# Local layers of a fused transformer block on one core: k projected ahead of q, two small operations moved from POOL to DVE, and the output block moved behind the scores

## The chip, the core and the metric

The kernel runs on one core of a Trainium2 chip. A core has five engines that work through their own queues: TensorE (PE) for matrix products and transposes, VectorE (DVE), ScalarE (ACT), GpSimd (POOL), and SyncE (SP), which here only issues DMAs. An instruction starts when those before it in its queue allow it and when the semaphores it waits for are set, so one late instruction holds everything behind it in the same queue. The metric is the device time of one execution in microseconds; the time before is 1243.0 us, the median of three runs (1241.72 to 1243.09).

## The reference

The input is x of 4 x 1024 x 128 in fp32. Two blocks follow each other, each with an attention part and a feed-forward part under an adaptive layer norm. Block 0 has a linear attention and a routed mixture of 16 experts; the attention of block 1 looks at a window of 64 keys and a prefix of 16. The change touches the feed-forward part of block 1, which is itself a stack of two small transformer layers with local attention (8 heads of 64, window 64). Cut to what matters:

```python
for l in range(2):
    h = shift_token(x)
    q, k, v = split(h @ wqkv[l])                       # 3 x 512 columns, 8 heads of 64
    q = q / clip(norm(q), 1e-12) * q_scale[l]
    k = k / clip(norm(k), 1e-12) * k_scale[l]
    q, k = rotary_xpos(q, k)                           # q*cos + rotate_half(q)*sin, scaled by position
    sim = einsum("bhwid,bhwjd->bhwij", q * 8, look_around(k))
    attn = softmax(where(mask, -max, sim))
    x = x + (attn @ look_around(v)) @ wo[l]
    h = layernorm(shift_token(x)) * ln_g[l] + ln_b[l]
    a, g = split(h @ w1[l] + b1[l])
    x = x + (a * gelu(g)) @ w2[l] + b2[l]
```

The l2 norm of every head is what the change is about: a sum of 64 squares for each token and head, a maximum with a small number, and a power of -1/2.

## The kernel before

The tokens are cut into tiles of 128, eight to a sequence, so the two local layers have 2 x 4 x 8 = 64 tiles. They run from about 579 us to the end. Ahead of them come block 0 (to about 330 us) and the window attention of block 1 (to about 579 us); in the last iterations of the latter the first three tiles of the local layers are projected already, one of six projections (three tiles, q and k) per iteration (line 821).

PE's order is the order of the program (`manual_schedule(engines={PE})`). The order on DVE, ACT and POOL is planned at build time: an instruction goes into its engine's queue when the planner thinks it ready, earlier ones in the program first. So the queues of these three follow the program loosely, and moving a line can reorder them.

A tile of the local layers goes through these functions:

- `project` (line 645; w = 0 is q, w = 1 is k): PE multiplies 128 tokens with 512 columns (L653). ACT squares the result (L656), DVE makes two products, `co` with the cosines (L658) and `si` with the sines (L663), and sums the squares by head into `ss[:, w]` (L665, 128x8). POOL adds `co` and `si` (L673). When w is 1, POOL also takes the maximum of both halves of `ss` (L668, 128x16), raises them to -1/2 (L669, 128x16), and multiplies k's `co` by k's half (L675). The eight squared norms of q and of k so share one power, taken when the second of them, k, is there. q's half is not multiplied into q; it is the scale in the masking of the scores (L892).
- `turn`: PE transposes q or k (L845); ACT copies q to `qT` (L852), DVE copies k into `kT` (L858). For the first sequence of the first layer (`light`), q's sum is left to PE, which adds two products with the identity (L849).
- `values`: PE projects v (L864), ACT copies it, and SP shifts it by half a tile with two DMAs into `ve`.
- `scores`: 32 small products (L885); DVE masks them, scales them by q's half of `ss`, and keeps each row's least value (L892, eight instructions); ACT takes the exponentials and their sums (`exps`, L904).
- `over_sums`: DVE takes the reciprocals (L912); POOL normalizes one half of the weights and DVE the other (L919).
- `flip`: PE transposes the weights (L926), ACT copies them to `pt` (L928).
- `outputs`: PE multiplies them with v and `ve` (L940, 32 products), ACT copies the result to `os` (L944).
- Side steps, spread over the iterations: the projection of the outputs (`project_out`, L951), the layer norm in front of the MLP (`mlp_in`, `mlp_out`), and the MLP (`mlp_gate` L986, `mlp_up` L995 and L997, `mlp_down` L1003).

PE's matmul results lie in eight banks: two for scores, six for everything else in the local layers. A bank is free again when its last reader is done.

In iteration g of the loop (line 1064) PE's order is: scores of tile g, q's projection of tile g+2, first flip of tile g-2, k's projection of tile g+2, second flip of tile g-2, turn of q of tile g+1, outputs of tile g-3, turn of k of tile g+1, then side steps and the values of tile g-1. For 1 < g < 7 the turn of q stands ahead of the first flip.

Every layer norm goes through `ln_in` (line 133): DVE takes mean and variance (L144, L146) and subtracts the mean (L150); POOL adds epsilon to the variance (L152, 128x4), raises to -1/2 (L153) and multiplies (L154). There are 49 of them in the whole kernel, most of them in block 0 and the window attention.

Of the kernel before, what the change touches and what calls it, by code (L numbers as in the profile page):

```python
# [22 lines left out]
ALU = mybir.AluOpType  # L23
# [3 lines left out]
P = 128  # L27
# [9 lines left out]
HEADS, DH, DEPTH = 8, 64, 2  # L37
# [11 lines left out]
def adaln_blocks(ctx: ExitStack, tc: tile.TileContext, a: dict, out: bass.AP):  # L49
    nc = tc.nc  # L50
    pe, act, dve, pool = nc.tensor, nc.scalar, nc.vector, nc.gpsimd
# [4 lines left out]
    def const(name, shape, dtype=F32):  # L56
        return cp.tile(shape, dtype, tag=name, name=name)
# [5 lines left out]
    def bc(ap, shape):  # L63

        return ap.unsqueeze(len(ap.shape)).to_broadcast(shape)
# [39 lines left out]
    nhalf = const("nhalf", [P, 4])  # L105
# [27 lines left out]
    def ln_in(tp, src, wp, name, bufs=None, n=4):  # L133

        if src is not None:
            for i in range(4):
                pe.transpose(tp[:, i, :], src[:, i * P : (i + 1) * P], ident)
        tps = tp if isinstance(tp, list) else [tp]
        h, w = len(tps), D // len(tps)
        st = wp.tile([P, 4, 2, 6], F32, tag="st", name=f"st_{name}")  # L140
        mv = wp.tile([P, 4, 2], F32, tag="mv", name=f"mv_{name}")
        for i in range(n):
            for e in range(h):
                dve.bn_stats(st[:, i, e, :], tps[e][:, i, :])  # L144
        for i in range(n):
            dve.bn_aggr(mv[:, i, :], st[:, i, 0:h])  # L146

        xh = wp.tile([P, 4, D], F32, tag="xh", name=f"xh_{name}", bufs=bufs)
        for e in range(h):
            dve.tensor_tensor(xh[:, 0:n, e * w : (e + 1) * w], tps[e][:, 0:n], mv[:, 0:n, 0:1].to_broadcast([P, n, w]), ALU.subtract)  # L150
        rv = wp.tile([P, 4, 1], F32, tag="rv", name=f"rv_{name}")
        pool.tensor_scalar(rv[:, 0:n], mv[:, 0:n, 1:2], 1e-5, None, ALU.add)  # L152
        pool.tensor_tensor(rv[:, 0:n], rv[:, 0:n], nhalf[:, 0:n].unsqueeze(2), ALU.pow)  # L153
        ln_in.last = pool.tensor_tensor(xh[:, 0:n], xh[:, 0:n], rv[:, 0:n].to_broadcast([P, n, D]), ALU.mult)  # L154
        return xh
# [53 lines left out]
    NG8 = B * NT  # L209
# [390 lines left out]
    def const1(name, shape):  # L600
        return c1.tile(shape, F32, tag=name, name=name)

    wl = []
    for l in range(DEPTH):
        w = [const1(f"wqkv_{l}", [P, 3, HEADS * DH]), const1(f"wo_{l}", [P, 4, D]), const1(f"w1_{l}", [P, 2 * HID]), const1(f"w2_{l}", [P, 3, D])]
# [38 lines left out]
    late = {}  # L644
    pj = ctx.enter_context(tc.tile_pool(name="pj", bufs=3))

    def project(l, b, t, w, ps):


        nt = f"{l}_{b}_{t}_{w}"  # L650
        if w == 0:
            late[l, b, t, "ss"] = pj.tile([P, 2, HEADS], F32, tag="ss", name=f"ss_{nt}", bufs=4)
        pe.matmul(ps, lhsT=hs[l, b][:, t * P : (t + 1) * P], rhs=wl[l][0][:, w, :], start=True, stop=True)  # L653
        ph = ps.rearrange("p (h e) -> p h e", e=DH)
        sq = pj.tile([P, HEADS, DH], F32, tag="sq", name=f"sq_{nt}", bufs=2)
        act.activation(sq, ph, AF.Square)  # L656
        co = pj.tile([P, HEADS, DH], F32, tag=f"co{w}", name=f"co_{nt}")
        dve.tensor_tensor(co, ph, abs_[l][:, 0, t, w, :].unsqueeze(1).to_broadcast([P, HEADS, DH]), ALU.mult)  # L658
        si = pj.tile([P, HEADS, DH], F32, tag="si", name=f"si_{nt}", bufs=3)

        ex = bass.AP(tensor=ps.tensor, offset=ps.offset + 32, ap=[ps.ap[0], [DH, HEADS], [-32, 2], [1, 32]])
        sn = abs_[l][:, 1, t, w, :].rearrange("p (i e) -> p i e", i=2).unsqueeze(1).to_broadcast([P, HEADS, 2, 32])
        dve.tensor_tensor(si.rearrange("p h (i e) -> p h i e", i=2), ex, sn, ALU.mult)  # L663
        ss = late[l, b, t, "ss"]
        dve.tensor_reduce(ss[:, w, :], sq, AX.X, ALU.add)  # L665
        if w == 1:

            pool.tensor_scalar(ss, ss, 1.0e-24, None, ALU.max)  # L668
            pool.tensor_tensor(ss, ss, nhalf[:, 0:2].unsqueeze(2).to_broadcast([P, 2, HEADS]), ALU.pow)  # L669
        if w == 0 and light(l, b, t):  # L670
            late[l, b, t, "si"] = si
        else:
            pool.tensor_tensor(co, co, si, ALU.add)  # L673
        if w == 1:
            pool.tensor_tensor(co, co, bc(ss[:, 1, :], [P, HEADS, DH]), ALU.mult)  # L675
        late[l, b, t, "co", w] = co

    def light(l, b, t):

        return (l, b) == (0, 0) and t >= EARLY  # L680
# [5 lines left out]
    with (  # L686
# [28 lines left out]
        def weights(b, t):  # L715

            sv, mx = kept1[b, t, "s"]
            for j in range(4):
                if (b, t) != (0, 0):
                    maximum(b, t, j)  # L720
                mj = mx[:, 4 * j : 4 * j + 4]
                pr = kept1[b, t, "pr", j] = wp.tile([P, 4, KV], F32, tag="pr", name=f"pr_{b}_{t}_{j}", bufs=8)
                if j < 3:
                    dve.tensor_tensor(pr, sv[j], bc(mj, [P, 4, KV]), ALU.add)
                    act.activation(pr, pr, AF.Exp)
                else:
                    for h in range(4):
                        act.activation(pr[:, h, :], sv[j][:, h, :], AF.Exp, bias=mj[:, h : h + 1])
# [61 lines left out]
        def when(g, f, *args):  # L790
            if 0 <= g < NG8:
                f(*divmod(g, NT), *args)

        for g in range(-1, NG8 + 2):
            b, t = divmod(g, NT)
            ahead = 0 <= b and b + 1 < B
            if g == -1:
                weights(0, 0)
            when(g + 2, scores)
            when(g + 2, weights)  # L800
            if ahead and t in (2, 4):
                queries(b + 1, t // 2 - 1)
            for after, k, f in ((6, 0, tokens), (8, 0, normed), (11, 1, tokens), (13, 1, normed)):
                if (g - after) % NT == 0 and 0 <= (g - after) // NT < B - 1:
                    f((g - after) // NT, k, "h3")
            for at, k, f in ((1, 0, tokens), (3, 0, normed), (5, 1, tokens), (7, 1, normed)):
                if g == at:
                    f(B - 1, k, "h2")
            when(g - 1, back)
            when(g + 1, flip, (0, 1))  # L810
            when(g + 1, values)
            when(g, outputs)
            when(g + 1, flip, (2, 3))
            if t == 5 and 0 < b <= DEPTH:
                rotary(tab, abs_[b - 1], b - 1)
            if g % 4 == 1 and g > 4:
                project_out((g - 5) // NT, (g - 5) % NT // 4)
            if ahead and t in (3, 5):
                keys(b + 1, t // 2 - 1)

            for i, w in ((0, 0), (0, 1), (1, 0), (1, 1), (2, 0), (2, 1))[max(0, g - NG8 + 6) : max(0, g - NG8 + 7)]:
                project(0, 0, i, w, ps.tile([P, BLK], F32, tag="t", name=f"qk_0_0_{i}_{w}", bufs=2))

    both.close()
# [4 lines left out]
    with (  # L829
# [198 lines left out]
        for l in range(DEPTH):  # L1028
            for b in range(B):
                g = (l * B + b) * NT  # L1030
# [29 lines left out]
        def project_mid(l, b, t, w):  # L1060
            if (l, b) != (0, 0) or t >= EARLY:
                project(l, b, t, w, pM.tile([P, BLK], F32, tag="mid", name=f"qk_{l}_{b}_{t}_{w}"))

        for g in range(-1, tiles + 4):
            side = steps.get(g, [])
            when(g, scores)
            when(g + 2, project_mid, 0)

            turns = {-1: (0, 1), 0: (2,), 1: ()}.get(g, (g + 1,))
            if 1 < g < NT - 1:  # L1070
                when(g + 1, turn, 0)
            when(g - 2, flip, 0)
            when(g - 1, over_sums)
            when(g + 2, project_mid, 1)
            when(g - 2, flip, 1)
            when(g, exps)
            for i in turns:
                if not 1 < g < NT - 1:
                    when(i, turn, 0)
                if i < EARLY and g < EARLY:  # L1080
                    when(i, turn, 1)
            when(g - 3, outputs)
            if g >= EARLY - 1:
                when(g + 1, turn, 1)
            for f, args in side[:1]:
                f(*args)

            for i in {0: (), 1: (0,)}.get(g, (g - 1,)):
                when(i, values)

            f0 = g - 7
            if f0 % 4 == 0 and 0 <= f0 < tiles - NT:
                lo = f0 % NT * P
                project_out(f0 // (B * NT), f0 // NT % B, lo, lo + BLK)
            for f, args in side[1:]:
                f(*args)
# [127 lines left out]
```

## Time and profile before

| | us |
|---|---|
| time before, median of three runs | 1243.0 |
| the profiled execution | 1246.33 |
| its span | 1244.5 |
| block 0 | 0 to about 330 |
| window attention | about 330 to 579 |
| local layers, start | 579 to 692 |
| local layers, steady part | 692 to 1193 |
| last tiles and last MLP blocks | 1193 to 1244.5 |

One profiled execution gives a page and a trace of all its instructions. In the page, the first lines give the busy time of each engine with its share of the span; PEld is the loading of weights, which overlaps with PE. The groups of instructions read: line, engine, operation, result <- operands, shapes, how often; then the busy time in us and the mean of one in ns; then how long the engine sat idle just before them and what ended that. The busy time by stretch gives, for a window of the span, how long each engine was busy in it. The chain of waits is followed back from the end: each piece is an instruction that the next one waited for, by a semaphore or because it stood ahead of it in its queue. The timeline has every instruction with its start and its duration in us.

### The profile page before, as it was taken

To read this page: it belongs to the slowest core of one execution; us is meant where nothing else is said; L and a number is where in the kernel's file an instruction comes from. 1 tells how busy PE (TensorE), PEld (TensorE's weight loads), DVE (VectorE), ACT (ScalarE), POOL (GpSimd) and SP (SyncE) were. 2 spreads that over 40 slices of the span, in tenths; PEclk is the share of its full clock that TensorE was granted. 3 is DMA by queue.
4 is the path that set the end of the run, shared out by engine and by line. 5 is a ranking of instruction groups with operands and counts; after the bars stand their busy time and mean duration, and the time that the engine had idled before them with its cause. 6 is when DMAs were issued, how large, how long until landed. Compare 5 with 4: busy or idle time off the path is not lost.

```text
span 1244.5 us, 34772 instructions
## 1 busy us (share of the span) xinstructions
PE 1162.8 (93%) x13578; PEld 714.7 (57%) x13578; DVE 878.8 (71%) x2798; ACT 817.8 (66%) x2223; POOL 823.3 (66%) x813
## 2 busy tenths in 40 slices
PE   6789999999899999988898999999999999999998
PEld 5644453534476667755665556665555556565564
DVE  5556263452476667666878988898898888998864
ACT  3363373322577677766886788788877887788862
POOL 4436445746334445444889988888899889888840
PEclk8699999999999999999999999999999999999999
DMA  6040404021400000000112111111111111111110
GB/s 179 1 130 8 138 0 132 7 74 63 137 4 4 3 20 14 11 3 3 35 27 48 27 35 26 32 40 27 39 28 34 39 29 45 38 27 31 36 40 26
DMA packets 36136, 51.04 MB, mean 41 GB/s; under 512 B 5850, under 2 KB 17668, under 8 KB 35844
## 3 DMA queue, kind: packets, MB, share of 16 engines
q1 hardware_dynamic: 35540, 48.29, 14.1%
q8 instruction: 107, 1.75, 0.6%
q10 hardware_dynamic: 432, 0.53, 0.1%
q14 instruction: 57, 0.47, 0.1%
HBM read 26.52 MB, written 2.36 MB: 23 GB/s over the span
## 4 chain that ended last, share of the span: by engine, by line
PE 43%; DVE 27%; ACT 18%; POOL 7%; issue 5%; DMA 1%; POOLq 0%; ACTq 0%; SPq 0%; DVEq 0%
ACT pr L904 5%; PE h L489 4%; PE yp L951 4%; DVE pr L892 3%; DVE co L658 3%; PE s L885 3%; DVE si L663 3%; DVE ss L665 3%; PE ptr L735 3%; PE qk L653 3%; POOL u L494 2%; ACT sq L656 2%; PE s L261 2%; PE obank L752 2%; DVE ge L997 2%
## 5 line engine op out<-in xcount | busy, mean ns | idle before, releaser
L904 ACT ACTIVATE pr<-pr,mx 128x128 f32<-128x128 f32 x512 | 200.8, 403 | 88.2 <-DVE mx L892 88.1
L673 POOL TENSOR_TENSOR co<-co,si 128x512 f32<-128x512 f32 x123 | 156.7, 1280 | 79.5 <-DVE si L663 72.2
L669 POOL TENSOR_TENSOR ss<-ss,nhalf 128x16 f32<-128x16 f32 x64 | 191.7, 2995 | 5.3
L892 DVE CUSTOM_DVE_ANT_0 pr<-s,masks,ss 128x128 f32<-128x128 f32 x512 | 144.2, 342 | 42.4 <-PE s L885 42.0
L653 PE MATMUL qk<-wqkv,hs 128*128 128x512 f32 x256 | 137.7, 620 | 4.9 <-ACT pt L737 4.9
L494 POOL TENSOR_TENSOR u<-u,cw 128x512 f32<-128x512 f32 x64 | 81.1, 1271 | 74.4 <-ACT u L492 74.4
L489 PE MATMUL h<-hT,w 128*128 128x512 f32 x256 | 123.8, 605 | 4.0 <-DVE g L496 4.0
L496 DVE TENSOR_TENSOR g<-u,h 128x512 f32<-128x512 f32 x64 | 43.8, 686 | 114.9 <-POOL u L494 114.9
L279 DVE TENSOR_REDUCE mx<-s 128x4 f32<-128x448 f32 x128 | 73.5, 617 | 56.4 <-PE s L270 56.4
L658 DVE TENSOR_TENSOR co<-qk,ab 128x512 f32<-128x512 f32 x128 | 86.7, 677 | 26.0 <-ACT sq L656 26.0
L904 ACT ACTIVATION_READ_ACCUMULATOR pr<-pr,mx 128x1 f32 x512 | 101.7, 199 | 0.0
L492 ACT ACTIVATE u<-h 128x512 f32<-128x512 f32 x64 | 38.2, 598 | 93.2 <-PE h L489 85.7
L926 PEld LDWEIGHTS ptr<-ident,pr 128*128 128x128 f32 x512 | 63.5, 141 | 61.6 <-issue 54.8
L663 DVE TENSOR_TENSOR si<-qk,ab 128x512 f32<-128x512 f32 x128 | 86.8, 678 | 0.0
L489 PEld LDWEIGHTS h<-hT,w 128*128 128x128 f32 x256 | 48.3, 194 | 66.2 <-issue 51.0
L665 DVE TENSOR_REDUCE ss<-sq 128x8 f32<-128x512 f32 x128 | 86.2, 673 | 0.0
L656 ACT ACTIVATE sq<-qk 128x512 f32<-128x512 f32 x128 | 74.9, 586 | 14.8 <-PE qk L653 12.3
L845 PE MATMUL qktr<-ident,co 128*128 128x128 f32 x492 | 76.9, 280 | 6.6 <-POOL co L675 5.3
L885 PEld LDWEIGHTS s<-kT,qT 64*64 64x64 f32 x2048 | 56.8, 134 | 45.6 <-issue 22.1
L919 POOL TENSOR_TENSOR pr<-pr,sm 128x512 f32<-128x512 f32 x64 | 74.7, 1168 | 7.9 <-DVE sm L912 7.9
L885 PE MATMUL s<-kT,qT 64*64 64x128 f32 x2048 | 72.1, 277 | 7.6 <-DVE kT L858 6.1
L737 ACT COPY pt<-ptr 112x512 f32<-112x512 f32 x128 | 72.5, 612 | 8.6 <-PE ptr L735 8.6
(212 smaller groups left out, 2871.2 us busy)
## 6 DMA issues: line engine op xcount, KB each, us to landing
cw<-cd SPq DMA_DIRECT2D x128, 128.0 KB, 3.0
ve<-vs SPq DMA_DIRECT2D x120, 128.0 KB, 2.3
hs<-hT SPq DMA_DIRECT2D x16, 256.0 KB, 3.2
out<-out SPq DMA_DIRECT2D x7, 256.0 KB, 2.7
xin<-in_x SPq DMA_DIRECT2D x3, 512.0 KB, 6.1
w<-in_w SPq DMA_DIRECT2D x3, 512.0 KB, 5.0
wqkv<-in_wqkv SPq DMA_DIRECT2D x2, 768.0 KB, 5.3
ab<-in_tab SPq DMA_DIRECT2D x1, 1024.0 KB, 7.3
```

Source lines behind the costliest of these rows:

```text
L489: pe.matmul(h, lhsT=w[:, c * P : (c + 1) * P], rhs=hT[b][:, blk(k)], start=True, stop=True)
L494: pool.tensor_tensor(u, u, kept[b, k, "cw"][:, c, :], ALU.mult)
L653: pe.matmul(ps, lhsT=hs[l, b][:, t * P : (t + 1) * P], rhs=wl[l][0][:, w, :], start=True, stop=True)
L656: act.activation(sq, ph, AF.Square)
L658: dve.tensor_tensor(co, ph, abs_[l][:, 0, t, w, :].unsqueeze(1).to_broadcast([P, HEADS, DH]), ALU.mult)
L663: dve.tensor_tensor(si.rearrange("p h (i e) -> p h i e", i=2), ex, sn, ALU.mult)
L665: dve.tensor_reduce(ss[:, w, :], sq, AX.X, ALU.add)
L669: pool.tensor_tensor(ss, ss, nhalf[:, 0:2].unsqueeze(2).to_broadcast([P, 2, HEADS]), ALU.pow)
L673: pool.tensor_tensor(co, co, si, ALU.add)
L885: pe.matmul(S[j][qs, c, :], lhsT=q[rw, c, qs], rhs=k[rw, c, at : at + P], start=True, stop=True)
L892: dve.tensor_tensor_reduce(out=pr[:, c, :], in0=S[j][:, c, :], in1=mk[:, min(t, 1), :], scale=kept[l, b, t, "ss"][:, 0, h : h + 1], scalar ...
L904: act.activation(pr[:, c, :], pr[:, c, :], AF.Exp, bias=mx[:, j, c : c + 1], scale=-1.0, accum_out=sm[:, j, c : c + 1])
```

## The change

It does five things.

1. In `project`, the maximum moves from POOL to DVE and is taken for each half by itself, directly after the sum of squares (128x8, in place of one 128x16 on POOL). The power is taken for each half by itself, too (128x8): k's ahead of the sum of `co` and `si`, q's behind it.
2. k is projected ahead of q, in the loop of the local layers and for the three tiles that are projected early. The tile `ss` is made by whichever comes first.
3. `outputs` of tile g-3 moves from behind the turn of q to directly behind the scores of tile g.
4. So PE's order in iteration g becomes: scores of tile g, outputs of tile g-3, k's projection of tile g+2, first flip, q's projection, second flip, turn of q, turn of k, side steps, values.
5. In `ln_in`, the addition of epsilon moves from POOL to DVE.

```diff
@@ ln_in
         rv = wp.tile([P, 4, 1], F32, tag="rv", name=f"rv_{name}")
-        pool.tensor_scalar(rv[:, 0:n], mv[:, 0:n, 1:2], 1e-5, None, ALU.add)
+        dve.tensor_scalar(rv[:, 0:n], mv[:, 0:n, 1:2], 1e-5, None, ALU.add)
@@ project
-        if w == 0:
+        if (l, b, t, "ss") not in late:
             late[l, b, t, "ss"] = pj.tile([P, 2, HEADS], F32, tag="ss", name=f"ss_{nt}", bufs=4)
...
         dve.tensor_reduce(ss[:, w, :], sq, AX.X, ALU.add)
+        dve.tensor_scalar(ss[:, w], ss[:, w], 1.0e-24, None, ALU.max)
         if w == 1:
-
-            pool.tensor_scalar(ss, ss, 1.0e-24, None, ALU.max)
-            pool.tensor_tensor(ss, ss, nhalf[:, 0:2].unsqueeze(2).to_broadcast([P, 2, HEADS]), ALU.pow)
+            pool.tensor_tensor(ss[:, 1], ss[:, 1], nhalf[:, 0:1].to_broadcast([P, HEADS]), ALU.pow)
         if w == 0 and light(l, b, t):
             late[l, b, t, "si"] = si
         else:
             pool.tensor_tensor(co, co, si, ALU.add)
         if w == 1:
             pool.tensor_tensor(co, co, bc(ss[:, 1, :], [P, HEADS, DH]), ALU.mult)
+        else:
+            pool.tensor_tensor(ss[:, 0], ss[:, 0], nhalf[:, 0:1].to_broadcast([P, HEADS]), ALU.pow)
@@ the early projections
-            for i, w in ((0, 0), (0, 1), (1, 0), (1, 1), (2, 0), (2, 1))[max(0, g - NG8 + 6) : max(0, g - NG8 + 7)]:
+            for i, w in ((0, 1), (0, 0), (1, 1), (1, 0), (2, 1), (2, 0))[max(0, g - NG8 + 6) : max(0, g - NG8 + 7)]:
@@ the loop of the local layers
             when(g, scores)
-            when(g + 2, project_mid, 0)
+            when(g - 3, outputs)
+            when(g + 2, project_mid, 1)
...
             when(g - 1, over_sums)
-            when(g + 2, project_mid, 1)
+            when(g + 2, project_mid, 0)
             when(g - 2, flip, 1)
...
-            when(g - 3, outputs)
             if g >= EARLY - 1:
                 when(g + 1, turn, 1)
```

## Prediction

> **What bounds the kernel now.** The page first: PE is busy for 93% of the span, DVE for 71%, POOL and ACT for 66%. These shares average over stages, so the next view is the busy time by stretch. The change lies in the local layers, from 535 us on; from 692 to 1193 us their steady part runs.
>
> ```profile
> PE 1162.8 (93%) x13578; PEld 714.7 (57%) x13578; DVE 878.8 (71%) x2798; ACT 817.8 (66%) x2223; POOL 823.3 (66%) x813
> L673 POOL TENSOR_TENSOR co<-co,si 128x512 f32<-128x512 f32 x123 | 156.7, 1280 | 79.5 <-DVE si L663 72.2
> L669 POOL TENSOR_TENSOR ss<-ss,nhalf 128x16 f32<-128x16 f32 x64 | 191.7, 2995 | 5.3
> ```
>
> ```profile
> 645.00:692.00 47.00, 42.46 (x466) 27.20 (x464) 42.14 (x150) 34.90 (x118) 44.18 (x37) 1.00 0.16 36
> 692.00:1193.00 501.00, 496.37 (x4826) 298.99 (x4828) 433.69 (x1504) 396.33 (x1230) 439.53 (x352) 1.00 0.14 34
> ```
>
> The columns are window, length, then PE, weight loads, DVE, ACT, POOL, the granted clock and DMA. PE looks like the only bound (496.4 of 501), but DVE (433.7) and POOL (439.5) have some 13% left each, so the order decides. Scores start every 9.37, 10.08, 9.7 and 10.66 us, a cycle of 39.8 us for four tiles, since an MLP block is spread over four. The chain of waits through one cycle shows who sets it:
>
> ```profile
> 913.49 1.10 PE s L885 x32
> 920.78 3.43 PE yp L951 x8
> 924.22 1.10 PE s L885 x32
> 929.00 1.93 ACT pr L904 x10
> 937.30 0.49 ACT sq L656
> 937.82 0.69 DVE co L658
> 942.09 1.97 DVE ge L997 x3
> 952.58 0.61 DVE kT L858
> 953.32 1.10 PE s L885 x32
> ```
>
> PE leads for 11 us, then ACT to 937.8, then DVE without a gap to 953.2, where the copy of kT lets the next scores go. The loop is closed: what is added to DVE in those 15.4 us moves the next cycle. What is added where DVE waits anyway (1.5, 0.5, 2.1 and 0.8 us in this cycle's timeline) costs little.
>
> **The change, part by part.** The sum is made against the profiled execution: span 1244.5 us, 1246.3 with what lies around it, 3.3 above the median of 1243.0.
>
> *PE's order.* Scores take 1.03 us of PE, an output block 1.08. Behind the scores PE now runs the outputs, so the first projection starts 2.1 us after the scores instead of 1.03, the second 3.5 instead of 2.4; the turn of q moves from 3.7 to 4.8, k's stays at 5.3, and values and side steps follow as before. PE's work is unchanged. The outputs read tiles flipped one iteration and values made two iterations earlier: no new wait. The output's copy on ACT (0.48 us) moves ahead of the first square, to where ACT was late in the third tile (square at 937.30): 0 to 0.48 per cycle, I take 0.2, because an exponential or two stood ahead of that square before and can stand behind it now. SP's queue keeps its order: no DMA is issued by a moved step.
>
> *The power.* POOL loses 64 maxima of 0.26 us and one power of 128x16 (2.92), and gets two of 128x8. The rows have 128x4 at 1.04 and 128x16 at 2.92; the line between gives 1.67 each, so +0.42 - 0.33 = +0.1 us a tile. POOL has slack, so 0. k's product is ready after 1.67 instead of 2.92, and k's sums are 1.8 us of DVE earlier. Who waited for it: PE once for 3.0 us at 598 and about 1.3 us at 675 (the output block there took 2.41 for 1.08). I credit 3 us in all. Without that cover, it is worth nothing in the steady part: k is turned an iteration later.
>
> *The maximum on DVE.* This decides. 128 small operations (128x8, SBUF to SBUF) move to DVE, and 49 additions of epsilon (L152). Alone, such an operation advances DVE's queue by 0.07 (two at 9.75 take 0.24 together). But the trace shows what one does when POOL is busy with an elementwise product:
>
> ```profile
> 9.92 1.04 POOL L154 TENSOR_TENSOR xh_h<-xh_h,rv_h 128x512 f32<-128x512 f32 x1
> 9.96 1.02 DVE L125 TENSOR_SCALAR mag<-mod 128x4 f32<-128x4 f32 x1
> ...
> 179.20 1.26 POOL L494 TENSOR_TENSOR u<-u,cw 128x512 f32<-128x512 f32 x1 [4.17 <-ACT u L492]
> 179.58 0.92 DVE L431 TENSOR_SCALAR rank_g<-rank_g 128x32 f32<-128x32 f32 x1
> ...
> 754.90 2.92 POOL L669 TENSOR_TENSOR ss<-ss,nhalf 128x16 f32<-128x16 f32 x1
> 754.94 0.72 DVE L919 TENSOR_TENSOR pr<-pr,sm 128x512 f32<-128x512 f32 x1
> ...
> 939.02 0.68 DVE L665 TENSOR_REDUCE ss<-sq 128x8 f32<-128x512 f32 x1
> 939.25 1.27 POOL L673 TENSOR_TENSOR co<-co,si 128x512 f32<-128x512 f32 x1 [1.32 <-DVE si L663]
> ```
>
> A 0.16 us scalar operation took 1.02 and 0.92: it ended some 30 ns behind POOL's instruction. A power does not hold DVE so: L919, two SBUF inputs, ran 0.72 inside it, against 1.4 to 1.57 when it began in an addition of co. The last two lines are the place of the new maximum: POOL starts co + si when si is done, 0.2 us into the reduction, and runs until 940.52; the reduction ends at 939.70. A maximum directly behind it waits 0.82 us. Over the 98 reductions of the steady part the rest of POOL's instruction at that moment averages 0.73 us. So a maximum costs between 0.07 and 1.02; I take 0.5, below 0.73 because another DVE operation may be queued between reduction and maximum (as one is between L912 and L919 at 950), and because q's maximum often meets k's power. Behind it in DVE's queue stand the other projection's products, kT and the softmax; for those wait ACT, PE and POOL's power.
>
> [...]
>
> *The sum.* In the loop's DVE part (937.8 to 953.2) lie two tiles: four maxima at 0.5 = 2.0, one epsilon at 0.1 (POOL is near a power then), 0.2 for ACT: +2.3 a cycle. The other four maxima lie in the first two tiles, where DVE's waits (1.5 + 0.5 and 2.1 + 0.8) cover 1.0 each; without that cover they cost the same again. 501 / 39.8 = 12.6 cycles: +29 us. The light tiles (600 to 635, 8.57 us each): DVE waits 0.72 us for the second square (L656 at 615.03), which follows the second projection by PE's end plus 0.2; that projection comes 1.08 later, so +0.9, and one maximum ahead of kT +0.4: five periods, +6.5. From 635 to 692, seven tiles near DVE's and POOL's limit at 0.7 = +5. The six first projections (537 to 577): three reductions lie in the chain, with the addition of co beside them, 0.8 each: +2.5. The k's earlier delivery: -3, and about -4 for PE's small stalls that a cycle held (1.0 us of 39.8, a third of it from kT). The epsilon in the first 535 us: POOL's queue is 0.3 shorter for each of 32, DVE may be held up to 1.0; both are off the chain mostly: 0. Together +29 + 6.5 + 5 + 2.5 - 7 = +36: 1246.3 + 36 = 1282 for a profiled execution, 1279 against the median. At 0.25 a maximum the same terms give +16, 5.5, 3 and 1.5, less 7: +19, 1262; at 0.85 +47, 8, 8 and 2.5, less 7: +58, 1301.
>
> **The rivals.**
> - *The maxima miss POOL's additions* (the order of DVE's queue puts products between, or POOL is in powers). Then 0.07 each: 0.35 + 0.2 a cycle = 7, light tiles 5, gains -7 or less: about 1249. For it: DVE's order is planned, not fixed; against it: POOL is in an elementwise instruction 56% of the steady part.
> - *Faster: kT overtakes.* If kT's copy goes ahead of q's products in DVE's queue, scores no longer wait for DVE. It is worth PE's stalls, 1.0 a cycle = 12.6, and 0.53 in each of five light tiles (v takes 1.39 for 0.86): -15, 1228; 1233 with some of the maxima's cost. It decides where kT is turned: k's turn stays at 5.3 us while q's products can start at 4.5, so I give it little.
> - *Nothing moves:* stalls won and maxima lost cancel, 1243.
> [...]
>
> **How the numbers follow.** The forecast 1279 (1262 to 1301) has 0.54; small cost, 1249, 0.17; outright bound 0.09; no change 0.06; faster 0.14. A measurement of this kernel tells about 0.2% from no change. Faster 0.14, same 0.06, slower 0.80. The range leaves out most of the faster case and the worst of the last: 1238 to 1306.
>
> **What would show it.** The line of the new maximum with a median well above its minimum, near 0.5 to 0.9 beside a minimum of 0.16; cycles of about 42 us between every fourth scores; more DVE busy time by some 70 us; light tiles near 9.8; PE's share below 96% in the steady part, with waits for DVE's kT or si. Wrong is this if the maximum's median stays under 0.25, or if kT stands ahead of q's products on DVE and cycles stay below 40.

## The result, and the profile after

The changed kernel takes 1287.7 us, the median of six runs (1284.5 to 1293.9), against 1243.05 for the kernel before: a ratio of 1.0366, with a 95% interval from 1.0333 to 1.0399. It is slower by 3.7%. The profiled execution took 1285.8 us with a span of 1284.0, which is 39.5 more than the one before; the terms below are set against that difference.

The page after, with the lines that answer to those shown of the kernel before (group lines: busy us, mean ns of one | idle before, releaser):

```profile
PE 1166.7 (91%) x13578; PEld 724.3 (56%) x13578; DVE 959.2 (75%) x2975; ACT 819.2 (64%) x2223; POOL 815.3 (63%) x764
L672 POOL TENSOR_TENSOR co<-co,si 128x512 f32<-128x512 f32 x123 | 168.7, 1371 | 119.2 <-DVE si L663 114.2
L668 POOL TENSOR_TENSOR ss<-ss,nhalf 128x8 f32<-128x8 f32 x64 | 111.6, 1743 | 5.4
L676 POOL TENSOR_TENSOR ss<-ss,nhalf 128x8 f32<-128x8 f32 x64 | 110.5, 1727 | 1.8 <-DVE ss L666 1.3
```

DVE's busy time has grown by 80 us, PE's by 4 and POOL's has shrunk by 8. The same windows as before, after the change (window, length, PE, weight loads, DVE, ACT, POOL, granted clock, DMA):

```profile
645.00:692.00 47.00, 40.12 (x441) 26.32 (x440) 41.67 (x151) 30.87 (x106) 42.66 (x34) 0.93 0.17 38
692.00:1193.00 501.00, 467.89 (x4451) 286.80 (x4453) 457.30 (x1508) 373.30 (x1153) 413.76 (x318) 0.98 0.13 31
```

In the steady part PE is busy for 467.9 of 501 us where it was 496.4. The granted clock has fallen, too, from 1.00 to 0.98; that comes back below. What PE waits for before the scores shows in the waits from 692 to 1193 us (us in total, times, longest). The kernel before:

```profile
PEld s L885 <- issue: 19.9, 25, 1.1
PE s L885 <- DVE kT L858: 2.8, 11, 0.3
```

And the changed kernel:

```profile
PEld s L886 <- issue: 51.6, 30, 3.4
PE s L886 <- DVE kT L859: 30.1, 12, 2.6
```

Once in each cycle of four tiles, 12 times in the window, the scores now wait some 2.5 us for kT. It is the step in which `mlp_down` runs (I call it the MLP step; the step behind it is the fourth). The chain of waits of the changed kernel through that stall (start, us, what):

```profile
961.31 0.47 ACT os L945
961.78 0.51 ACT sq L656
962.31 0.69 DVE co L658
...
964.19 0.60 DVE co L658
964.79 0.26 DVE ss L666
965.04 0.59 DVE si L663
...
973.10 0.60 DVE co L658
973.71 0.60 DVE si L663
974.30 0.59 DVE ss L665
974.89 0.11 DVE sm L913
975.00 0.74 DVE ss L666
975.74 0.59 DVE co L658
976.33 0.93 DVE pr L920
977.26 0.60 DVE si L663
977.86 0.59 DVE ss L665
978.45 0.60 DVE kT L859
```

Both sums of squares and both pairs of products stand in one row ahead of kT, and the new maximum (L666) stands between k's sum and q's first product, with 0.74 us of its own.

By stages of the two profiled executions, where the 39.5 us are (first projection of the local layers at 537.0 before and 528.5 after):

| stretch | before | after | difference |
|---|---|---|---|
| up to the first projection | 537.0 | 528.5 | -8.5 |
| first projections to first scores | 44.3 | 48.1 | +3.8 |
| scores of tile 0 to tile 12 | 101.1 | 112.7 | +11.6 |
| scores of tile 12 to tile 60 (12 cycles) | 482.8 | 516.1 | +33.3 |
| from there to the last scores and out | 79.3 | 78.7 | -0.6 |

Most of the first line is the epsilon. PE runs the same 6446 matmuls ahead of the first projection in all fourteen kernels profiled here. From the 400th to the 800th, in block 0, they take 125.3 us in each of the eleven kernels with the epsilon on DVE, and 130.6 to 132.0 in the three with it on POOL: 5 to 7 us. The rest of the line I can give to no edit: in kernels that do not differ there, the 400th matmul starts between 134.5 and 138.5 us, and the time from the 800th to the first projection differs by up to 9 us.

### The profile page after: what moved, and what is told of

The parts are those of the page before. It is cut to its first block, busy times and chain, and to the rows that moved or that the text cites. A ratio compares the mean times of both kernels' runs of the same rounds, so it can differ in the third digit from the quotient of the medians.

```text
span 1284.0 us, 34792 instructions
## 1 busy us (share of the span) xinstructions
PE 1166.7 (91%) x13578; PEld 724.3 (56%) x13578; DVE 959.2 (75%) x2975; ACT 819.2 (64%) x2223; POOL 815.3 (63%) x764
## 4 chain that ended last, share of the span: by engine, by line
PE 42%; DVE 29%; ACT 18%; issue 5%; POOL 4%; DMA 1%; SPq 1%; POOLq 0%; ACTq 0%; DVEq 0%
ACT pr L905 5%; PE h L489 4%; PE yp L952 4%; DVE co L658 3%; DVE pr L893 3%; PE s L886 3%; DVE si L663 3%; PE qk L653 3%; DVE ss L665 3%; PE ptr L736 3%; PE o L941 2%; ACT sq L656 2%; PE s L261 2%; PE y L504 2%; DVE ge L998 2%
## 5 line engine op out<-in xcount | busy, mean ns | idle before, releaser
L672 POOL TENSOR_TENSOR co<-co,si 128x512 f32<-128x512 f32 x123 | 168.7, 1371 | 119.2 <-DVE si L663 114.2
L653 PE MATMUL qk<-wqkv,hs 128*128 128x512 f32 x256 | 144.2, 647 | 5.6 <-ACT pt L738 5.6
L886 PE MATMUL s<-kT,qT 64*64 64x128 f32 x2048 | 74.3, 283 | 49.8 <-DVE kT L859 39.8
L668 POOL TENSOR_TENSOR ss<-ss,nhalf 128x8 f32<-128x8 f32 x64 | 111.6, 1743 | 5.4
L676 POOL TENSOR_TENSOR ss<-ss,nhalf 128x8 f32<-128x8 f32 x64 | 110.5, 1727 | 1.8 <-DVE ss L666 1.3
L927 PE MATMUL ptr<-ident,pr 128*128 128x128 f32 x512 | 76.8, 274 | 0.0
```

The costliest lines, as they stand in the source:

```text
L668: pool.tensor_tensor(ss[:, 1], ss[:, 1], nhalf[:, 0:1].to_broadcast([P, HEADS]), ALU.pow)
L676: pool.tensor_tensor(ss[:, 0], ss[:, 0], nhalf[:, 0:1].to_broadcast([P, HEADS]), ALU.pow)
L886: pe.matmul(S[j][qs, c, :], lhsT=q[rw, c, qs], rhs=k[rw, c, at : at + P], start=True, stop=True)
L927: pe.transpose(tp[:, c, :], pr[:, c, :], ident)
```

## The experiments

Each kernel is timed against the kernel before on the same chip. That one's median was 1242.5 to 1245.6 from chip to chip, so between two rows the ratios say more than the medians. All of them in one table; the columns behind the ratio are from the profiled execution of each:

| kernel | median us | ratio (95%) | first projections | tiles 0-12 | tiles 12-60 |
|---|---|---|---|---|---|
| before | 1243.1 | 1 | 44.3 | 101.1 | 482.8 |
| changed | 1287.7 | 1.0366 (1.0333 to 1.0399) | 48.1 | 112.7 | 516.1 |
| 1 changed, maxima on POOL | 1255.7 | 1.0089 (1.0060 to 1.0119) | 44.2 | 107.9 | 491.0 |
| 2 changed, reciprocals for maxima | 1269.8 | 1.0212 (1.0174 to 1.0250) | 45.7 | 109.7 | 503.1 |
| 3 before, maxima on DVE | 1268.9 | 1.0195 (1.0167 to 1.0224) | 47.9 | 107.6 | 502.4 |
| 4 before, epsilon on DVE | 1241.9 | 0.9994 (0.9977 to 1.0011) | 44.3 | 101.4 | 486.2 |
| 5 before, outputs moved | 1252.0 | 1.0061 (1.0039 to 1.0082) | 44.0 | 108.4 | 485.9 |
| 6 k first, with the epsilon | 1246.8 | 1.0017 (1.0000 to 1.0035) | 44.2 | 102.9 | 487.8 |
| 7 changed, no maxima | 1255.4 | 1.0095 (1.0061 to 1.0128) | 47.0 | 107.1 | 490.3 |
| 8 changed, two reciprocals | 1274.7 | 1.0248 (1.0221 to 1.0274) | 45.5 | 110.6 | 506.7 |
| 9 changed, PE kept busy | 1279.3 | 1.0302 (1.0280 to 1.0324) | 47.4 | 111.5 | 510.5 |
| 10 changed, k's maximum alone on DVE | 1285.0 | 1.0340 (1.0313 to 1.0367) | 46.7 | 114.0 | 521.9 |
| 11 changed, q's maximum alone on DVE | 1257.8 | 1.0121 (1.0098 to 1.0144) | 48.4 | 108.3 | 491.7 |
| 12 as 10, PE kept busy | 1280.2 | 1.0269 (1.0234 to 1.0304) | 48.3 | 110.0 | 508.3 |

The first two questions: do the maxima make the loss, or the order? And if the maxima, is it their wait for POOL?

### 1. The maxima back on POOL

```diff
-        dve.tensor_scalar(ss[:, w], ss[:, w], 1.0e-24, None, ALU.max)
+        pool.tensor_scalar(ss[:, w], ss[:, w], 1.0e-24, None, ALU.max)
```

> The changed kernel with the maximum back on POOL (by halves, 128x8), everything else as changed. If the maxima on DVE are the loss (they wait for POOL's products: 128 of them, 36 us over their free 0.155 us in the trace of the changed kernel): 1245 to 1260, what stays being the output's copy ahead of the first square (0.5 us a cycle, 6 us) and the later second projection of the light tiles (5 us). If the order of PE is the loss: it stays above 1275.

1255.7 us: 32 of the 44 us go with this one line. The remaining 12 are the rest of the change, which experiments 4 to 6 take apart. PE in the steady part of this kernel is busy for 483.7 us instead of 467.9:

```profile
692.00:1193.00 501.00, 483.69 (x4711) 297.69 (x4709) 431.33 (x1479) 391.39 (x1206) 454.26 (x432) 1.00 0.14 33
```

### 2. A reciprocal in the place of each maximum

```diff
-        dve.tensor_scalar(ss[:, w], ss[:, w], 1.0e-24, None, ALU.max)
+        dve.reciprocal(ss[:, w], ss[:, w])
...
-            pool.tensor_tensor(ss[:, 1], ss[:, 1], nhalf[:, 0:1].to_broadcast([P, HEADS]), ALU.pow)
+            pool.tensor_tensor(ss[:, 1], ss[:, 1], phalf[:, 0:1].to_broadcast([P, HEADS]), ALU.pow)
...
-            pool.tensor_tensor(ss[:, 0], ss[:, 0], nhalf[:, 0:1].to_broadcast([P, HEADS]), ALU.pow)
+            pool.tensor_tensor(ss[:, 0], ss[:, 0], phalf[:, 0:1].to_broadcast([P, HEADS]), ALU.pow)
```

> The changed kernel with each maximum on DVE replaced by a reciprocal of the same 128x8 in the same place, the power then being +1/2: the clip at 1e-24 is left out. As many instructions on DVE, and POOL's power waits for them as before; but the reciprocals of L912 in the kernel before never took more than 0.204 us whatever POOL did. If waiting for POOL is the cause: within 6 us of the kernel with the maximum on POOL (128 x 0.08 = 10 us of DVE, half of it in the loop), 1250 to 1265. If the longer queue of DVE or the hop from DVE to POOL's power is the cause: 1280 or more.

1269.8 us, 5 above the range for waiting and 10 below that for a cost of place. The reciprocal never waits (median 0.194, longest 0.204 us, 128 times), so 18 of the 32 us are gone. For the other 14, the timeline of its MLP step (start, us, engine, line):

```profile
963.77 0.20 DVE L915 RECIPROCAL sm<-sm 128x8 f32<-128x8 f32 x1
963.89 0.20 DVE L668 RECIPROCAL ss<-ss 128x8 f32<-128x8 f32 x1
964.01 1.22 DVE L922 TENSOR_TENSOR pr<-pr,sm 128x512 f32<-128x512 f32 x1
...
965.15 0.68 DVE L660 TENSOR_TENSOR co<-qk,ab 128x512 f32<-128x512 f32 x1
```

The same place in the kernel of experiment 1:

```profile
958.25 1.27 POOL L672 TENSOR_TENSOR co<-co,si 128x512 f32<-128x512 f32 x1 [0.75 <-DVE si L663]
958.62 0.18 DVE L913 RECIPROCAL sm<-sm 128x8 f32<-128x8 f32 x1
958.74 0.63 DVE L658 TENSOR_TENSOR co<-qk,ab 128x512 f32<-128x512 f32 x1
959.29 0.78 DVE L920 TENSOR_TENSOR pr<-pr,sm 128x512 f32<-128x512 f32 x1
```

With one more instruction in the queue, the planner has put the normalization ahead of q's `co` instead of behind it. There it starts in POOL's addition and takes 1.22 us where it took 0.78; `co` took no longer beside the same addition: in the trace of the changed kernel the 57 that start in it take 0.677 to 0.686 us, and the 41 that start with POOL idle 0.691 to 0.694. So the wait that the maximum had is taken over in part by the normalization: the MLP step is 11.29 us, against 10.57 in experiment 1 and 11.82 to 11.88 in the changed kernel. Over the 12 cycles that is 8.6 of the 12.1 us by which tiles 12 to 60 are longer than in experiment 1; three stretches at half clock, which experiment 1 does not have there, come on top.

### 3. The maxima alone, in the kernel before

```diff
         dve.tensor_reduce(ss[:, w, :], sq, AX.X, ALU.add)
+        dve.tensor_scalar(ss[:, w], ss[:, w], 1.0e-24, None, ALU.max)
...
-            pool.tensor_scalar(ss, ss, 1.0e-24, None, ALU.max)
```

> The kernel before with nothing changed but the maxima, by halves on DVE. If they are the loss: +20 to +35, 1263 to 1278. If they only hurt together with the new order: +0 to +10.

1268.9 us, +1.95%, as expected: the maxima cost most of it in the old order too. Its light tiles, 8.57 us each before, take 8.57, 8.57 and 8.88: there the maxima are covered.

### 4. The epsilon alone

```diff
-        pool.tensor_scalar(rv[:, 0:n], mv[:, 0:n, 1:2], 1e-5, None, ALU.add)
+        dve.tensor_scalar(rv[:, 0:n], mv[:, 0:n, 1:2], 1e-5, None, ALU.add)
```

> The kernel before with nothing changed but the epsilon of the layer norms on DVE. The changed kernel reaches its first local scores 4.7 us earlier (576.6 for 581.3). If that is the epsilon: -3 to -6, 1237 to 1240. If it is the order of the early projections: within 2 us of 1243.

No difference in the whole time: 0.9994 with an interval that holds 1. In the profiled execution two effects stand against each other. Block 0 is faster by the 5 to 7 us given above; one place in it, in the kernel before (start, us, engine, line, idle before):

```profile
226.94 0.63 PE L137 MATMUL in_h<-ident,xT 128*128 128x128 f32 x4 [2.46 <-DVE xh_h L150]
```

The same place here, and the epsilon in the MLP step of a cycle:

```profile
220.42 0.63 PE L137 MATMUL in_h<-ident,xT 128*128 128x128 f32 x4 [0.35 <-DVE xh_h L150]
898.74 0.37 DVE L152 TENSOR_SCALAR rv_m<-mv_m 128x4 f32<-128x4 f32 x1
```

The local layers are slower: there the epsilon starts in POOL's product with k's norms, takes 0.37 us, and pushes the row ahead of kT back by 0.28. From the second cycle on the MLP step is 9.95 to 10.09 us for 9.66 to 9.74, and tiles 12 to 60 take 3.4 us more.

### 5. and 6. The outputs' place alone, and k ahead of q alone

Experiment 5, in the kernel before:

```diff
             when(g, scores)
+            when(g - 3, outputs)
             when(g + 2, project_mid, 0)
...
-            when(g - 3, outputs)
             if g >= EARLY - 1:
```

> The kernel before with only the outputs moved directly behind another tile's scores. With the maxima back on POOL the changed kernel took 1255.7 us, 12 above the kernel before: its cycle of four tiles was 40.3 us for 39.8 and its light tiles 6.8 us longer in sum. If the place of the outputs makes those 12 us (the output copy of 0.47 us on ScalarE ahead of the first square in each cycle, and the second projection one output step later in the light tiles), this kernel takes 1250 to 1257 us. If k's projection ahead of q makes them, this kernel takes 1241 to 1246 us.

Experiment 6 is the changed kernel with that line back in its old place and the maxima on POOL:

```diff
             when(g, scores)
-            when(g - 3, outputs)
             when(g + 2, project_mid, 1)
...
+            when(g - 3, outputs)
             if g >= EARLY - 1:
...
-        dve.tensor_scalar(ss[:, w], ss[:, w], 1.0e-24, None, ALU.max)
+        pool.tensor_scalar(ss[:, w], ss[:, w], 1.0e-24, None, ALU.max)
```

> The changed kernel with the outputs back in their old place and the maxima on POOL: what is left is k ahead of q, k's power alone, and the epsilon on DVE. If the outputs' place makes the 12 us, this kernel takes 1238 to 1246 us, with scores that begin up to 5 us earlier after the first projections. If k's projection ahead of q makes them, it takes 1250 to 1257 us.

The outputs make +0.61% and k first +0.17%, together 0.78 of the 0.89% of experiment 1. 7.3 us of the outputs' cost lie in tiles 0 to 12: its light tiles take 9.90 us for 8.57, exactly as in the changed kernel and in experiment 1. In the steady part its cycle is 40.2 us for 39.8. Experiment 6 holds the epsilon's move too.

### 7. No maxima at all

```diff
-        dve.tensor_scalar(ss[:, w], ss[:, w], 1.0e-24, None, ALU.max)
```

> The changed kernel without the maxima: the clip of the sums of squares from below is left out, on every engine. If the 32 us between the changed kernel and the one with the maxima on POOL come from an instruction standing in DVE's queue between a tile's reduction and the work behind it, this kernel takes what that one took, 1250 to 1259 us, and the normalization on DVE is back at 0.80 to 0.90 us in the mean. If it is DVE's other work that has come to meet POOL's additions in the new order, the normalization stays above 1.1 us and the time above 1265.

The time was as the first theory had it, 1255.4. Its second mark failed: the normalization is not back below 0.9 us. The line of the kernel without maxima:

```profile
L919 DVE TENSOR_TENSOR pr<-pr,sm 128x512 f32<-128x512 f32 x59 | 73.7, 1249 | 1.3
```

And of the kernel with the maxima on POOL:

```profile
L920 DVE TENSOR_TENSOR pr<-pr,sm 128x512 f32<-128x512 f32 x59 | 50.6, 857 | 1.3
```

23 us more of DVE's time in waiting, and the same time of the kernel. In the MLP step of both, the normalization takes 0.8; the waits of 1.56 us stand in other steps, which are as long as before but for one (10.63 us for 10.51). So the sum of a line's waits is no price; only those in the chain ahead of kT are.

### 8. Two reciprocals

```diff
-        dve.tensor_scalar(ss[:, w], ss[:, w], 1.0e-24, None, ALU.max)
+        dve.reciprocal(ss[:, w], ss[:, w])
+        dve.reciprocal(ss[:, w], ss[:, w])
```

> The changed kernel with two reciprocals, one behind the other, in the place of each maximum; the second undoes the first, so that the power stays as it is, and the clip from below is left out. One reciprocal of 0.194 us, which never waited, took the time to 1269.8 us, 14 above the kernel with the maxima on POOL. If the price is an instruction's own length on DVE's path, another 0.19 us at each of 128 places adds 10 to 17 us: 1279 to 1287. If it came from a chance meeting of the normalization with POOL's additions, which another 0.19 us moves rather than adds to, the time stays at 1262 to 1275.

1274.7: just in the range of the second reading, with 1.0248 (1.0221 to 1.0274) for 1.0212 (1.0174 to 1.0250), two intervals that overlap. 128 more instructions of 0.196 us are 25 us of DVE's time, and some 0.4% came out. The MLP step says it more clearly: it grew by 0.20, from 11.29 to 11.49, where the first reciprocal had made it 0.72 longer, and the normalization still stands ahead of q's `co`. So what the first reciprocal cost was mostly the place it pushed the normalization to.

### 9. PE kept busy in the stall

In the changed kernel, in its cycles, the fourth step took 10.87 us in some and 12.03 to 12.11 in others, at the same work. The windows of the changed kernel show the clock (1.00 or 0.50, behind POOL's busy time):

```profile
934.00:937.41 3.41, 1.41 (x44) 1.26 (x46) 3.41 (x7) 0.10 (x1) 3.33 (x3) 1.00 0.33 77
937.41:940.83 3.42, 3.42 (x32) 2.17 (x27) 3.20 (x18) 1.74 (x7) 3.42 (x3) 0.50 0.02 5
974.96:978.38 3.42, 1.65 (x4) 0.38 (x2) 3.42 (x7) 1.70 (x6) 3.42 (x3) 1.00 0.00 1
978.38:981.79 3.41, 2.60 (x65) 2.20 (x66) 3.38 (x7) 0.00 (x0) 3.33 (x4) 1.00 0.34 81
```

PE busy for 1.41 of 3.41 us, and the next 3.4 us are granted half the clock; busy for 1.65, and they are not. To tell whether idleness itself does it, the values' projection was repeated into the same result where PE waits:

```diff
+            for _ in range(3 if t % 4 == 1 and (l, b) != (0, 0) else 1):
                 pe.matmul(ps, lhsT=hs[l, b][:, t * P : (t + 1) * P], rhs=wl[l][0][:, 2, :], start=True, stop=True)
```

> The changed kernel with the values' projection issued three times instead of once, each time over the same result, in every fourth tile from the seventeenth on: 1.7 us more of matmuls in the 2.75 us in which TensorE stands before the scores and waits for kT. The output is the same. In the changed kernel every stretch at half clock in the cycles follows 3.4 us in which TensorE was busy for less than half, and the step in that stretch takes 12.0 us instead of 10.87. If idleness itself sets the clock back, these stretches go, some 7 of them, and the time falls by 5 to 9 us to 1278 to 1283. If the clock goes by something else, or its halves cost nothing, the time stays at 1286 to 1290, and the stretches stay.

1279.3, as expected if idleness does it: with more work on PE the kernel is 8 us faster (1.0302 for 1.0366). Between 680 and 1205 us no stretch at half clock is left, where the changed kernel has seven, and tiles 12 to 60 take 510.5 for 516.1. The six runs of the changed kernel fit this: the shortest, 1284.5 us, had a mean granted clock of 0.976, and the two longest, 1293.8 and 1293.9, had 0.964 and 0.965. The steady part of this kernel:

```profile
692.00:1193.00 501.00, 486.07 (x4564) 292.43 (x4563) 461.37 (x1525) 374.72 (x1163) 418.22 (x322) 1.00 0.13 31
```

### 10. and 11. One maximum at a time

```diff
-        dve.tensor_scalar(ss[:, w], ss[:, w], 1.0e-24, None, ALU.max)
+        (dve if w else pool).tensor_scalar(ss[:, w], ss[:, w], 1.0e-24, None, ALU.max)
```

> The changed kernel with k's maximum on DVE and q's back on POOL. With both on POOL the kernel took 1255.7 us. In the step before the slow scores, k's maximum stands 0.73 us ahead of q's first product and the normalization behind it takes 0.22 us more: if the path runs through DVE's queue as read, that step is 0.95 us longer than its 10.57, the others are unchanged, and with 12.6 cycles the time is 1266 to 1272, with up to two stretches at half clock. A flat price for each maximum, whichever it is, would halve the 32 us: 1271 to 1274 here and with q's alone.

```diff
-        dve.tensor_scalar(ss[:, w], ss[:, w], 1.0e-24, None, ALU.max)
+        (pool if w else dve).tensor_scalar(ss[:, w], ss[:, w], 1.0e-24, None, ALU.max)
```

> The changed kernel with q's maximum on DVE and k's back on POOL. q's maximum stands behind kT; it pushes the work behind it, which delays the start of the slow step's first square by 0.33 us, and lengthens the step behind by 0.36: 0.69 us a cycle over 12.6 cycles on top of 1255.7, so 1262 to 1267. A flat price would give 1271 to 1274. The two maxima together with the stretches at half clock should make up the 32 us: 12 and 9, and the rest the clock.

Both missed, in opposite directions: k's maximum alone takes 1285.0, nearly all of the loss, and q's alone 1257.8, some 2 us. A flat price for each falls with that. The line with k's alone (duration min/median/max in ns):

```profile
L666 DVE TENSOR_SCALAR ss<-ss x64: 266/340/1154, 529.4 to 1224.8; 128x8 f32<-128x8 f32 x64
```

With q's alone:

```profile
L666 DVE TENSOR_SCALAR ss<-ss x64: 151/160/1851, 538.8 to 1192.4; 128x8 f32<-128x8 f32 x64
```

k's maximum always waits (its least is 266 ns): 62 of the 64 start while POOL is in the addition of `co`, which began inside the reduction ahead of them, and the other two start in a product of a layer norm. The MLP step with k's alone takes 11.74 to 11.88 us, as in the changed kernel but for 0.07, and the fourth step 10.86 where it is undisturbed, the changed kernel's own. I had given that second lengthening to q's maximum. But what q's maximum waits for in the changed kernel, 0.94 us behind kT, the normalization next in the queue waits for when the maximum is not there: 1.81 us instead of 0.96, and both end 2.47 us after the scores. In this step the wait for POOL's product is paid once, by whichever of the two meets it first.

What is left of the miss is the clock. With k's maximum alone four cycles hold stretches at half clock of 6.8 us instead of 3.4; its steps with such stretches took 13.4 us more than the same steps without. The profiled execution was the slowest of its four (1288.8 us, with a clock of 0.968; the others had 0.971 to 0.975), so the others lost less.

### 12. k's maximum alone, with PE kept busy

The edits of experiments 9 and 10 together.

> The changed kernel with k's maximum on DVE, q's on POOL, and the values' projection issued three times in every fourth tile from the seventeenth on, as in the kernel that kept TensorE busy. k's maximum alone took 1285.0 us; the steps behind its stalls held stretches at half clock that took 13.4 us together above the undisturbed length of the same steps (12.0 to 13.4 us for 10.86 four times a cycle's length apart, and less in the last cycles). If those 13 us are the clock and the rest the queue, this kernel takes 1269 to 1274 us and its slow step still takes 11.8. If k's maximum costs them in another way, the time stays at 1281 or more.

The time, 1280.2, is above the range for that reading and just below the other. In the stretch that the reading was about it holds: tiles 12 to 60 take 508.3 us instead of 521.9, and the MLP step still 11.75 to 11.87. The rest of the two profiled executions goes both ways: the first projection begins 4.6 us later (nothing of this edit runs ahead of it), the first projections take 1.6 more, tiles 0 to 12 take 4.0 less, and the last tiles 1.6 more, where a repeated product has no stall to hide in. So the clock's 13.5 us in the cycles are shown for the execution of experiment 10 that was profiled, its slowest; by the ratios the whole time fell by 0.7%, some 9 us.

## Why the prediction was right

The forecast was 1279, the measured time 1287.7, within the range and in the case that it called likeliest: small operations on DVE that wait for POOL's products, in a loop that DVE closes. Point by point:

- **The maximum waits for POOL's products: right, and closely.** In the changed kernel 82 of the 128 maxima start while POOL is in an addition, a product or its half of the normalization, and all 82 end 26 to 34 ns behind the end of POOL's instruction. Of the normalization's 59 on DVE, 50 start so, and all end 545 to 552 ns behind it. The timeline of the stall:

```profile
974.23 0.67 DVE L665 TENSOR_REDUCE ss<-sq 128x8 f32<-128x512 f32 x1
974.45 1.27 POOL L672 TENSOR_TENSOR co<-co,si 128x512 f32<-128x512 f32 x1 [1.03 <-DVE si L663]
974.82 0.18 DVE L913 RECIPROCAL sm<-sm 128x8 f32<-128x8 f32 x1
974.93 0.81 DVE L666 TENSOR_SCALAR ss<-ss 128x8 f32<-128x8 f32 x1
...
978.84 1.04 POOL L674 TENSOR_TENSOR co<-co,ss 128x512 f32<-128x512 f32 x1
978.97 0.94 DVE L666 TENSOR_SCALAR ss<-ss 128x8 f32<-128x8 f32 x1
```

  974.93 + 0.81 is 975.74; POOL's addition ends at 975.72.
- **0.5 us for each maximum: too much for most, and not what mattered.** The line of the changed kernel has them:

```profile
L666 DVE TENSOR_SCALAR ss<-ss x128: 152/284/1667, 532.2 to 1223.9; 128x8 f32<-128x8 f32 x128
```

  The median is 0.284, below the 0.5 to 0.9 that the prediction named as its mark and not far above the 0.25 under which it called itself wrong; the mean is 0.437, of which 0.155 is the operation when nothing is in its way. What failed is the step that took one price and counted four of them into the loop. The queue of DVE decides for each: k's maximum in the MLP step costs its full 0.8, in other steps another product stands between and it costs 0.26, and q's mostly takes a wait that the normalization had before.
- **+2.3 us a cycle: nearly right, by other terms.** A cycle with an undisturbed clock takes 41.9 us (9.21 + 9.99 + 11.82 + 10.87) against 39.8. Of these +2.1, +0.5 is the order with the epsilon (40.28 in experiment 1) and +1.6 the maxima. In the MLP step from experiment 1 to the changed kernel it is +1.31: 0.32 since k's first product starts later, 0.73 for the maximum (7.61 to 8.34 us into the step), and 0.22 for the normalization behind it (0.92 for 0.70); these make 1.27. The other +0.36 is in the fourth step. That four maxima at one price came to nearly the same sum is luck.
- **The output's copy on ACT at 0.2: undersized.** The cycle with the outputs moved alone is 0.4 longer, near the upper end that was given (0.48): its MLP step is 0.8 longer (10.50 us), the three other steps together 0.4 shorter. That the copy is the cause is not shown: in that MLP step the first exponential starts 2.87 us behind the scores, where the copy on ACT ends at 2.82, and DVE's first minimum, which it needs as well, at 2.83.
- **Light tiles at 9.8: 9.9, but for one reason, not two.** The prediction put 0.9 on the outputs' place and 0.4 on a maximum. The outputs' place alone gives 9.90, the maxima alone 8.57. The term of the maxima there is 0. Only three steps took 8.57 us, not the five that the sum counted, so they make 4.0 of its 6.5 us; the two steps ahead of them grew by 0.9 and 2.0, and tiles 0 to 12 as a whole by 11.6, where the sum had 11.5 up to 692 us.
- **The first projections, +2.5: +3.8.** 47.9 us with the maxima alone and 44.2 with the changed order and the maxima on POOL speak for the maxima, but the kernel without any has 47.0. The clock has a part in it: in the five kernels with 44.0 to 44.3 no stretch at half clock falls there, in eight of the other nine 3.4 to 9.5 us do, and 6.8 in the changed kernel. How much of the 3.8 is the maxima's is not settled.
- **Seven us back from an earlier k and smaller stalls: not there.** k first without the outputs' move gives +0.17% (0.00 to 0.35) and not less, and PE's waits for kT rose from 2.8 to 30.1 us in the steady part. This is the step that put the sum too low, together with the next one: from the first projection on the kernel grew by 48 us where the sum had 36, and the 7 us and the clock's 5.6 to 8 make up that difference.
- **The clock was not in the sum.** A stall that the sum priced at its length cost another 1.2 us where the clock fell behind it, 5.6 us from tile 12 to 60 and some 8 in all by experiment 9.
- **The epsilon at 0 up to 535 us and 0.1 a cycle: the whole right (0.9994), the parts not.** It won 5 to 7 us in block 0, and alone it cost 0.28 in a cycle (3.4 us over tiles 12 to 60). In the changed kernel its median in the local layers is 0.15 us: there it does not wait. So the first part made good some of what the sum had missed from the first projection on, and that the whole came within 9 us of the forecast is in part luck.

The other marks were met: cycles of 41.9 us and, with a stretch at half clock, 43.2 (about 42), 80 us more of DVE (70), light tiles of 9.9 (9.8), PE at 93% of the steady part (under 96), and the waits for kT.

Of the rivals, the cheap maxima (1249) and nothing moving (1243) are out by the result. "kT overtakes" needed kT ahead of q's products; the chain shows it behind them. For the outright bound, at 0.09, POOL's powers would have had to hold DVE as well, and no run shows that: one maximum and six normalizations ran wholly inside a power of the changed kernel, and took 0.159 and 0.681 to 0.693 us, where those that began with POOL idle took 0.157 to 0.162 and 0.692 to 0.693; DVE was busy for 457.3 of 501 us in the steady part.

From the table the parts of tiles 12 to 60 add up so: 482.8 before, +8.2 for the order and the epsilon (experiment 1, 491.0), +19.5 for the maxima (experiment 9, 510.5), +5.6 for the clock (516.1). No kernel here beats the one before; the nearest are the epsilon alone (0.9994) and k first with the outputs in their old place (1.0017).

What stays open is how the epsilon's place shortens block 0, what else moves the first projection by several us between profiled executions, and why the maxima cost 25 us in the old order and 32 in the new: the old order's cycles show no stretch at half clock, which covers 5.6 of the difference, and the rest is within the intervals.

## What to carry to other kernels

Price a small instruction by what stands beside it on the other engine at the very place in the queue where it will run, not by a mean over its kind: here one of two equal maxima cost nearly everything (1285.0 us with k's alone on DVE) and the other almost nothing (1257.8 with q's alone, 1255.7 with neither). A wait that is taken away or left out can be taken over by the next instruction in the queue (the normalization went from 0.78 to 1.22 us in experiment 2), and waits off the chain cost nothing here (23 us more of them in experiment 7, at 1255.4 us for 1255.7), so read the chain and not the sum of a line's waits. And when a change opens a stall on TensorE, look at the granted clock in the 3.4 us behind it before the stall's length is taken for its price (here it fell to 0.50 behind some of the stalls, and in five cycles the step took 12.03 to 12.11 us for 10.87).

## What the runs showed of the hardware that was not expected

**The clock of TensorE falls behind a stall, and by a grid.** In each run the changes of the granted clock lie on one grid of 3.413 us, whose phase differs from run to run. Over the fourteen profiled executions, from 560 to 1225 us, 49 cells of the grid went from full to half clock. In the cell before, PE was busy for 0.54 of the time at most, and for 0.48 or less in 46 of them. Some 2600 cells stayed at full clock, and none of the cells before them was busy for less than 0.44. The way back takes more: after a cell at half clock the clock came back in 49 cases, all with PE busy for 0.87 or more in that cell, and stayed at half in 8, all at 0.82 or less (five of those in the kernel with k's maximum alone, four of them in its cycles). So a stall of 2.7 us did or did not cost 1.2 us more, by where it lay in the grid, in about every second cycle.

**One instruction of 128x8 waits for POOL, another does not.** In the changed kernel the 128x8 maximum ended 26 to 34 ns behind POOL's instruction in all 82 cases in which it began within an addition or a product; the 128x8 reciprocal in the same place, and in the same tile, took 0.156 to 0.204 us in all of the 128 cases of experiment 2. Why the one waits and the other does not, no run here tells.
